# Four graph layers on one core: messages in three bfloat16 parts, one layer turned through DRAM, a new order

## The chip, the cores and the metric

The kernel runs on one core of one Trainium2 chip. The metric is device time in microseconds (us) from the first to the last instruction of one execution. A core has a matrix engine (TensorE, PE in the profile), a vector engine (VectorE, DVE), a scalar engine (ScalarE, ACT), a general engine (GpSimd, POOL) and a queue from which transfers are issued (SyncE, SP). They run side by side and wait for each other on semaphores. Matrix products read their operands from SBUF, the on-chip memory of 128 partitions, and leave their result in PSUM, eight banks of 128 x 512 float32, from where ACT or DVE copy it back.

## The reference

64 graphs of 256 nodes, 256 features each, pass through four layers. Each layer normalises, takes the positive part, runs a graph layer on it and adds the result to x:

```python
h = jnp.maximum(_layernorm(x, axis=-1), 0.0)
x = x + layer(h, adj, ...)
```

Layer 0 is attention of 8 heads, layer 1 attention with one score per edge and a softmax over the other axis, layer 3 attention of 4 heads. Layer 2 is a gated graph network of three rounds, which the change touches most:

```python
A = (adj != 0).astype(x.dtype)
h = x
for i in range(3):
    m = jnp.einsum('bnd,de->bne', h, weight[i])
    aggr = jnp.einsum('bst,bsd->btd', A, m)
    h = _gru_cell(aggr, h, w_ih, w_hh, b_ih, b_hh)
# _gru_cell, with gi = aggr @ w_ih.T + b_ih and gh = h @ w_hh.T + b_hh in three parts:
r = sigmoid(i_r + h_r); z = sigmoid(i_z + h_z)
n = tanh(i_n + r * h_n)
h = (1.0 - z) * n + z * h
```

Everything is float32. The adjacency comes as int32 and holds 0 and 1.

## The kernel before

The kernel works on pairs of graphs, 32 of them, T = 4 tiles of 128 nodes each. Every step is a task with the tiles that it reads and writes, the engines that could do it and an estimated duration; a planner (class Plan) walks through the tasks as a list scheduler would, gives each a place in the order of an engine and a buffer of its pool, and several pairs are thereby in work at once. Only the order comes from it: on the chip, the semaphores decide.

```python
SPARE, GRAIN = 4, 0.001
PERIOD, REST = 138.279, 1.02081
ON_PE = (-212.355, -45.5106, 229.667, -1085.75)      # by layer, added to a task's key
...
base = t.rank[0] * self.PERIOD - rest * self.REST + t.rank[1] * 1e-4
...
key = (round(begin / self.GRAIN), t.key, t.index)    # the ready task with the least key is next
```

Pools, with the number of buffers and how many are kept for the oldest pair: "x" (6, 0), "w4" (28, 9) of 128 x 1024 float32, "mask" (4, 1) of 128 x 1024 bfloat16, "ps" (8, 2), the PSUM banks.

A matrix product needs features on the partitions, the normalisation nodes, so tiles are turned. There are two ways. PE turns 128 x 128 blocks into a bank, and ACT or DVE copy it out. Or DVE turns 32 x 32 blocks in place, and a transfer to DRAM and four back put the blocks where they belong; the tile that comes back is "mixed": the eight 128-blocks lie interleaved, element by element, with steps of 8 float32.

```python
def by_dma(what, p):
    return 0 < p < B // 2 - 1

def through_dram(e, eT):
    d = buf("turn")
    add((SP, 0.6, lambda: nc.sync.dma_start(d(), e())), reads=[e], writes=[d], latency=4.6)
    for b in range(4):
        add((SP, 0.55, ...), reads=[d], writes=[(eT, b)], latency=3.8)

def chunk(hT, k, t):
    if hT.mixed:
        return hT().rearrange("p (n x) -> p x n", x=2 * T)[:, T * k + t]
    ...
```

In the middle 30 pairs the normalised tile of all four layers goes through DRAM (with the scaling and the positive part on ACT, L522), and so does the state between the rounds of layer 2. In the first and last pair DVE scales (L527), PE turns (L542), and the positive part is taken in the copy out of the bank.

Layer 2's messages multiply the state by the adjacency, both float32 (the loaded int32 adjacency is turned into float32 in place):

```python
for o in range(2):
    ps = bank()
    def product(o=o, ps=ps):
        for g in range(2):
            for c in range(2):
                t = 2 * g + c
                mm(ps()[:, g * N : (g + 1) * N], chunk_of(h, t, o), tok(am(), N)[:, t, :],     # L934
                   start=c == 0, stop=c == 1)
```

In rounds 0 and 1 the part h_n stays in its PSUM bank until r is known (pshn): tanh of the half on ACT (L969), then on DVE r = 0.5 * tanh + 0.5 (L974), then (h_n + b) * r out of the bank (L978). The gates' products are L957, those of the last round L1047.

Layer 1 adds its turned mask to the scores on DVE (L856), takes the row maximum (L861), and ACT takes the exponential (L590). Layers 0 and 3 do addition and minimum in one fused DVE step (`lowered`, L655), whose exponentials are L663. The softmax rows of layer 0 are divided on ACT or DVE (L745), its value projection and output projection are L576, layer 1's projection L820, layer 3's L1129; layer 3 spreads a row through DRAM to all partitions (`to_all`), takes Prelu rows (L1150), and multiplies by the turned probabilities (L1172), whose result is turned back (L1187).

Of the kernel before, what the change touches and what calls it, by code (L numbers as in the profile page):

```python
# [9 lines left out]
FP = mybir.dt.float32  # L10
# [12 lines left out]
class Buf:  # L23


    def __init__(self, tag, tiles):
        self.tag, self.tiles, self.slot, self.parts = tag, tiles, None, {}
        self.woven = False
        self.mixed = False
# [9 lines left out]
class Plan:  # L39
# [14 lines left out]
    SPARE, GRAIN = 4, 0.001  # L54
    PERIOD, REST = 138.279, 1.02081
    ON_PE = (-212.355, -45.5106, 229.667, -1085.75)
    ON_SP = (1007.6, 146.333, -62.4427, 928.914)
    OTHERS = (294.968, 127.685, -2183.49, 1293.66)
# [47 lines left out]
    def order(self):  # L106
# [11 lines left out]
        for t in reversed(every):  # L118
            rest = max((x.rest + 0.2 for x in t.after), default=0.0) + min(f[1] for f in t.forms) + t.latency
            t.rest = rest  # L120
            base = t.rank[0] * self.PERIOD - rest * self.REST + t.rank[1] * 1e-4
            engine = t.forms[0][0]
            t.key = base + (self.ON_PE if engine == "PE" else self.ON_SP if engine == "SP" else self.OTHERS)[t.layer]
# [9 lines left out]
        while ready:  # L133
            best = None
            for t in ready:
                start = 0.0
                new = [b.tag for b in t.bufs if b.slot is None]
                for tag in set(new):
                    n = new.count(tag)
                    have = slots[tag]  # L140
                    if len(have) < n + (spares.get(tag, 0) if t.pair != oldest else 0):
                        break
                    start = max(start, have[n - 1][0])
                else:
                    for form in t.forms:
                        engine = form[0]
                        begin = max(start, free.get(engine, 0.0), free.get("port", 0.0) if len(form) > 3 else 0.0)
                        for x in t.before:
                            begin = max(begin, x.end + (self.HOP if x.engine != engine else self.SAME)[x.engine])
                        key = (round(begin / self.GRAIN), t.key, t.index)  # L150
                        if best is None or key < best[0]:
                            best = (key, t, form, begin)
# [9 lines left out]
            t.end, t.engine = begin + us + t.latency, engine  # L162
# [19 lines left out]
def tile_adj_preln_d4(  # L182
# [41 lines left out]
        "x": (6, [P, T * D], FP, 0),  # L224
        "w4": (28, [P, T * D], FP, 9),
# [40 lines left out]
    brz, bih_sb, bhh_sb = held("brz", [P, 4]), held("bih_sb", [P, 6]), held("bhh_sb", [P, 6])  # L266
# [19 lines left out]
    def w4():  # L286
        return buf("w4")
# [91 lines left out]
    def weights2():  # L379
# [45 lines left out]
        def halved():  # L425
            nc.vector.tensor_add(brz, bih_sb[:, 0:4], bhh_sb[:, 0:4])
            nc.vector.tensor_scalar_mul(brz, brz, 0.5)

# [55 lines left out]
    def by_dma(what, p):  # L484

        return 0 < p < B // 2 - 1

    def norm_relu_T(xt, p, tokens=False):
# [15 lines left out]
        def rstd():  # L504
            nc.gpsimd.tensor_scalar_add(rs()[:, 0, :], mv()[:, :, 1], EPS)  # L505
            nc.gpsimd.tensor_tensor(rs()[:, 0, :], rs()[:, 0, :], mhalf, ALU.pow)

        add((G, 1.4, rstd, True), reads=[mv], writes=[(rs, 0)])
        xn, mixed = w4(), by_dma(plan.layer, p)
        relu = tokens or mixed  # L510
        if relu:
            add(
                (V, 0.17, lambda: nc.vector.scalar_tensor_tensor(  # L513
                    rs()[:, 1, :], mv()[:, :, 0], -1.0, rs()[:, 0, :], ALU.mult, ALU.mult)),
                reads=[mv, (rs, 0)], writes=[(rs, 1)],
            )
        for g in range(2):

            def scaled(g=g):
                for t in (2 * g, 2 * g + 1):  # L520
                    if relu:
# [10 lines left out]
            add((A, 0.95, scaled) if relu else (V, 0.7, scaled, True), reads=[(xt, g), mv, rs], writes=[(xn, g)])  # L532
# [4 lines left out]
        for k in range(2):  # L537
            ps = bank()

            def turn(k=k, ps=ps):  # L540
                for t in range(T):
                    nc.tensor.transpose(ps()[:, t * P : (t + 1) * P], tok(xn())[:, t, k * P : (k + 1) * P], ident)  # L542

            add((PE, 4 * TURN, turn), reads=[xn], writes=[ps], claims=[hT])
            dst = lambda k=k: tok(hT(), N2)[:, k, :]
            if tokens:
                add(evict(N2, dst, ps), reads=[ps], writes=[(hT, k)])
            else:
                add(
                    [  # L550
                        (A, act(N2), lambda dst=dst, ps=ps: nc.scalar.activation(dst(), ps(), AF.Relu)),
                        (V, dve(N2), lambda dst=dst, ps=ps: nc.vector.tensor_scalar_max(dst(), ps(), 0.0)),
                    ],
                    reads=[ps], writes=[(hT, k)],
                )
# [29 lines left out]

    def exp_group(e, mx, zs, parts, nm):

        def do():
            for i, m, z in parts:
                nc.scalar.activation(  # L590
                    tok(e(), N)[:, i, :], tok(e(), N)[:, i, :], AF.Exp,
                    bias=mx()[:, m : m + 1], accum_out=zs()[:, z : z + 1],
                )
        return (A, 0.494 * len(parts), do)
# [190 lines left out]
    def to_all(row, src, columns, n, dsts):  # L785
# [8 lines left out]
            (SP, 0.7, lambda: nc.sync.dma_start(row().rearrange("(c p) -> c p", p=P), rows()[0:n, :])),  # L794
# [11 lines left out]
    def layer1(xt, p):  # L806
# [45 lines left out]
        for g in range(2):  # L852
            two = slice(2 * g, 2 * g + 2)
            parts = [(e, 2 * g), (e, 2 * g + 1)]
            add(
                (V, dve(N2), lambda two=two: nc.vector.tensor_tensor(  # L856
                    tok(e(), N)[:, two, :], tok(e(), N)[:, two, :], psm()[:, two, :], ALU.add)),
                reads=[psb], writes=parts,
            )
            add(  # L860
                (V, dve(N2), lambda two=two: nc.vector.tensor_reduce(  # L861
                    mx()[:, two], tok(e(), N)[:, two, :], AX.X, ALU.max, negate=True)),
                reads=parts, writes=[(mx, g)],
            )
            add(exp_group(e, mx, zs, [(i, i, i) for i in (2 * g, 2 * g + 1)], f"1_{p}"), reads=[(mx, g)], writes=[*parts, (zs, g)])
# [39 lines left out]
    def layer2(xt, p):  # L905
        at, hT, h = norm_relu_T(xt, p, tokens=True)
        am = at
        add(
            (V, dve2(T * N), lambda: nc.vector.tensor_scalar(am(), am().bitcast(I32), 0.0, None, ALU.not_equal), True),
            reads=[hT], writes=[am],  # L910
# [8 lines left out]
        def chunk_of(h, t, o):  # L919
            if h.mixed:  # L920
                return h().rearrange("p (m x) -> p x m", x=2 * T)[:, T * o + t]
            return tok(h())[:, t, o * P : (o + 1) * P]

        def messages(h):
            aT = w4()
            aT.woven = woven
            for o in range(2):
                ps = bank()

                def product(o=o, ps=ps):  # L930
                    for g in range(2):
                        for c in range(2):
                            t = 2 * g + c
                            mm(  # L934
                                ps()[:, g * N : (g + 1) * N], chunk_of(h, t, o), tok(am(), N)[:, t, :],
                                start=c == 0, stop=c == 1,
                            )

                add((PE, 1.9 if h.mixed else 1.76, product), reads=[h, am], writes=[ps], claims=[aT])
# [6 lines left out]
        for l in range(NL - 1):  # L946
# [16 lines left out]
            pshn = [gate(1.72, ((whhT, hT),), (4 + o) * P, o, [r, hn]) for o in range(2)]  # L963
            aT = messages(h)
            both = ((whhT, hT), (giT[:, l], aT))
            for o in range(2):
# [7 lines left out]
                    (V, dve2(N2), lambda o=o, r=r: nc.vector.tensor_scalar(at_o(r, o), at_o(r, o), 0.5, 0.5, ALU.mult, ALU.add), True),  # L974
                    writes=[(r, o)],
                )
                add(
                    (V, dve(N2) + 0.07, lambda o=o, ps=pshn[o], r=r, hn=hn: nc.vector.scalar_tensor_tensor(  # L978
                        at_o(hn, o), ps(), bhh_sb[:, 4 + o : 5 + o], at_o(r, o), ALU.add, ALU.mult)),
                    reads=[pshn[o], (r, o), BN], writes=[(hn, o)],  # L980
# [138 lines left out]
    def layer3(xt, p):  # L1119
        at, hT = norm_relu_T(xt, p)  # L1120
        mb = buf("mask")
        add((V, 2 * dve2(N2), lambda: masked_keys(mb, at, ALU.not_equal, 1.0), True), reads=[at, hT], writes=[mb])
        f = buf("f3")
        for t in range(T):
# [6 lines left out]
            add((PE, 0.96 if hT.mixed else 0.9, product), reads=[hT, W3], writes=[ps], claims=[f])  # L1131
# [6 lines left out]
        add(  # L1138
            (V, 0.09, lambda: nc.vector.tensor_copy(dst(), f()[:, :, D + H3 : E3]), True), reads=[f], writes=[dst]
        )  # L1140
        to_all(buf("row3"), dst, lambda: dst().rearrange("p t h -> p (t h)"), T * H3, sd)
# [58 lines left out]

    for p in range(B // 2):
# [8 lines left out]
        if p == 0:  # L1210
            for plan.rank, weights in ((None, weights0), (0.5, weights1), (1.5, weights2), (2.5, weights3)):
                weights()
            plan.rank = None
# [43 lines left out]
```

## Time and profile before

| | before |
|---|---|
| time, median of 3 | 3811.62 us (3810.75 to 3811.85) |
| span of the profiled execution | 3809.6 us |
| busy PE, DVE, ACT, POOL | 3703.2, 3140.9, 2282.9, 687.5 us |
| messages L934: matmul records, mean duration | 1536, 398 ns |
| block turns on DVE for normalised tiles and states (L630) | 360, 1110 ns each |
| writes of tiles to be turned to DRAM, 512 KB each | 564 |
| DMA over the span | 743.00 MB, mean 195 GB/s |

The page gives each engine's busy time and its share of the span. A line such as L934 is a line of the kernel before. In a table of groups the columns are: line, engine, operation, tiles out and in, shapes, count; then total busy time and mean duration in ns; then the idle time of the engine ahead of these instructions, and who ended it. Matmul durations overlap, since the engine is pipelined, and a float32 product leaves two records; transposes leave one. In a timeline the columns are start, duration, engine, line and so on, with idle time ahead of the row in brackets. A table of stretches gives, for each, its length, then busy time and instructions of each engine, the granted PE clock, the DMA share and GB/s.

### The profile page before, as it was taken

To read this page: it belongs to the slowest core of one execution; us is meant where nothing else is said; L and a number is where in the kernel's file an instruction comes from. 1 tells how busy PE (TensorE), PEld (TensorE's weight loads), DVE (VectorE), ACT (ScalarE), POOL (GpSimd) and SP (SyncE) were. 2 spreads that over 40 slices of the span, in tenths; PEclk is the share of its full clock that TensorE was granted. 3 is DMA by queue.
4 is the path that set the end of the run, shared out by engine and by line. 5 is a ranking of instruction groups with operands and counts; after the bars stand their busy time and mean duration, and the time that the engine had idled before them with its cause. 6 is when DMAs were issued, how large, how long until landed. Compare 5 with 4: busy or idle time off the path is not lost. (4 is left out here: it accounts for less than half of the span.)

```text
span 3809.6 us, 54273 instructions
## 1 busy us (share of the span) xinstructions
PE 3703.2 (97%) x15632; PEld 2423.5 (64%) x15632; DVE 3140.9 (82%) x8350; ACT 2282.9 (60%) x6061; POOL 687.5 (18%) x635
## 2 busy tenths in 40 slices
PE   7999999999999999999999999999999999999995
PEld 4665766666666656666666666666666666766663
DVE  7998888788888768888879978898888898887565
ACT  5776556565575655665656656556656556655444
POOL 2001221112211112121221121221111221121121
PEclk9999999999999999999999999999999999999997
DMA  8766574666765757567576666666676676665434
GB/s 266 223 196 198 163 230 159 199 214 179 231 216 158 220 155 217 183 197 235 165 219 206 203 198 185 213 217 195 199 218 201 202 223 198 200 208 161 125 100 127
DMA packets 531801, 743.00 MB, mean 195 GB/s; under 512 B 54704, under 2 KB 446768, under 8 KB 531504
## 3 DMA queue, kind: packets, MB, share of 16 engines
q1 hardware_dynamic: 531504, 739.53, 63.1%
q8 instruction: 126, 2.06, 0.2%
q14 instruction: 171, 1.40, 0.1%
HBM read 426.52 MB, written 312.80 MB: 194 GB/s over the span
## 5 line engine op out<-in xcount | busy, mean ns | idle before, releaser
L663 ACT ACTIVATE w<-w,mx 128x256 f32<-128x256 f32 x1536 | 757.4, 497 | 32.3 <-DVE mx L655 32.0
L957 PE MATMUL ps<-w,whhT 128*128 128x512 f32 x1536 | 710.5, 595 | 1.2 <-ACT w L316 0.8
L957 PE MATMUL ps<-w,giT 128*128 128x512 f32 x1536 | 710.0, 593 | 0.0
L316 ACT COPY w<-ps 128x512 f32<-128x512 f32 x400 | 335.9, 846 | 353.8 <-PE ps L687 86.2
L957 PEld LDWEIGHTS ps<-w,giT 128*128 128x128 f32 x1536 | 290.1, 190 | 348.8 <-issue 333.6
L957 PEld LDWEIGHTS ps<-w,whhT 128*128 128x128 f32 x1536 | 286.8, 191 | 302.7 <-issue 281.8
L621 DVE STREAM_TRANSPOSE w<-w 128x1024 f32<-128x1024 f32 x384 | 460.9, 1223 | 9.4 <-ACT w L663 7.1
L655 DVE CUSTOM_DVE_ANT_0 w<-ps,mask 128x256 f32<-128x256 f32 x1024 | 368.6, 418 | 108.1 <-PE ps L714 105.7
L630 DVE STREAM_TRANSPOSE w<-w 128x512 f32<-128x512 f32 x360 | 374.4, 1110 | 39.3 <-ACT w L522 36.6
L934 PE MATMUL ps<-w,w 128*128 128x256 f32 x1536 | 381.0, 398 | 2.9 <-DMA w<-turn 2.3
L934 PEld LDWEIGHTS ps<-w,w 128*128 128x128 f32 x1536 | 346.8, 280 | 52.5 <-issue 26.0
L1047 PE MATMUL ps<-whhT,w 128*128 128x512 f32 (+1 forms) x1024 | 374.8, 502 | 0.3 <-DVE w L1012 0.3
L1047 PE MATMUL ps<-giT,w 128*128 128x512 f32 (+1 forms) x1024 | 364.0, 495 | 0.6 <-ACT w L316 0.6
L522 ACT ACTIVATE w<-x,rs 128x256 f32<-128x256 f32 x488 | 254.1, 589 | 163.5 <-DVE rs L513 144.3
L1047 PEld LDWEIGHTS ps<-giT,w 128*128 128x128 f32 x1024 | 276.1, 310 | 73.2 <-issue 8.5
L1047 PEld LDWEIGHTS ps<-whhT,w 128*128 128x128 f32 x1024 | 274.0, 311 | 70.8 <-issue 12.2
L663 ACT ACTIVATION_READ_ACCUMULATOR w<-w,mx 128x1 f32 x1536 | 291.6, 190 | 0.0
L1102 POOL TENSOR_TENSOR w<-w,w 128x512 f32<-128x512 f32 x64 | 101.7, 1594 | 1051.8 <-DMA w<-turn 477.2
L994 POOL TENSOR_TENSOR w<-w,w 128x512 f32<-128x512 f32 x128 | 178.7, 1402 | 461.2 <-ACT w L989 406.1
L1150 ACT ACTIVATE w<-w,f 128x256 f32<-128x256 f32 x512 | 216.8, 498 | 27.0 <-DMA w<-row 24.2
L505 POOL TENSOR_SCALAR rs<-mv 128x4 f32<-128x4 f32 x128 | 36.6, 286 | 971.9 <-DVE mv L497 855.9
L655 DVE CUSTOM_DVE_ANT_0 w<-w,mask 128x256 f32<-128x256 f32 x512 | 192.5, 421 | 20.5 <-ACT w L1150 20.5
(120 smaller groups left out, 5706.0 us busy)
## 6 DMA issues: line engine op xcount, KB each, us to landing
turn<-w SPq DMA_DIRECT2D x564, 512.0 KB
w<-turn SPq DMA_DIRECT2D x2256, 128.0 KB
w<-in_adj_dram SPq DMA_DIRECT2D x128, 512.0 KB
w<-row SPq DMA_DIRECT2D x64, 512.0 KB
x<-in_x_dram SPq DMA_DIRECT2D x64, 256.0 KB
out_dram<-x SPq DMA_DIRECT2D x64, 256.0 KB
w<-row SPq DMA_DIRECT2D x32, 256.0 KB
w<-in_L_gnn_weight_dram SPq DMA_DIRECT2D x3, 256.0 KB
```

The source lines that it names most:

```text
L316: (A, act(n), lambda: nc.scalar.copy(dst(), src())),
L522: nc.scalar.activation(tok(xn())[:, t, :], tok(xt())[:, t, :], AF.Relu, bias=rs()[:, 1, t : t + 1], scale=rs()[:, 0, t : t + 1],)
L621: add((V, dve(T * N), lambda: nc.vector.transpose(blocks(), blocks())), writes=[e])
L630: nc.vector.transpose(e().rearrange("p (b i k t) -> p k b t i", b=4, i=32, k=2)[:, k], src().rearrange(f"p {order} -> p k b t j", b=4, j=3 ...
L655: nc.vector.tensor_tensor_reduce(row, src, mask, scale, 3.0e38, ALU.add, ALU.min, mn)
L663: nc.scalar.activation(row, row, AF.Exp, bias=mn()[:, r : r + 1], scale=-1.0, accum_out=zs()[:, z0(r) : z0(r) + 1])
L934: mm(ps()[:, g * N : (g + 1) * N], chunk_of(h, t, o), tok(am(), N)[:, t, :], start=c == 0, stop=c == 1,)
L957: mm(ps(), w[:, k, c0 : c0 + P], wide(src, k), start=n == 0, stop=n == 2 * len(terms) - 1)
L994: either(lambda eng, o=o, u=u, hT=hT, hn=hn: eng.tensor_sub(*((tok(at_o(u, o), T), wide(hT, o), tok(at_o(hn, o), T)) if hT.mixed else (at_ ...
L1047: mm(out, chunk(src, k, t), w[:, k, c0 : c0 + n], start=m == 0, stop=m == 2 * len(terms) - 1)
L1102: either(lambda eng, g=g: eng.tensor_sub(two(df, g).rearrange("p t (k m) -> p t k m", k=2), state(h, g), two(hn, g).rearrange("p t (k m) - ...
L1150: (A, act(N, 1), lambda t=t, g=g, h=h, e=e, r=r: nc.scalar.activation(rows_of(e())[:, r].rearrange("p b (c j) -> p c b j", c=2), sd[g]().r ...
```

## The change

It has five parts.

**Messages.** A float32 is split exactly into three bfloat16 parts: its own upper half, the upper half of what remains, and the upper half of what then remains. The adjacency of 0 and 1 is exact in bfloat16. Three bfloat16 products per chunk take the place of one float32 product. The parts are read in place with a step (`upper`), and two subtractions of 1024 elements on DVE make the remainders. The adjacency is now a bfloat16 "mask" tile.

**Turns.** Only layer 2's tile and its states go through DRAM, there for the first pair too; layers 0, 1 and 3 are turned on PE in all pairs.

**The gate n in rounds 0 and 1.** h_n is taken out of its bank at once as 0.5 * h_n + 0.5 * b, on ACT or DVE; then a single DVE step makes (tanh + 1) * that. L974 goes.

**Layer 1** uses the fused step for mask and minimum.

**Order.** New constants; latencies of transfers count 1.3 times in the plan; a task of SP counts 0.6 us later after another engine; a task with a choice of engines counts 1 us later on DVE and 1.1 us later on POOL; x has 5 buffers and w4 29. The last pair's layer 3 is prepared graph by graph ("fine"). Weights of later layers come at other ranks.

The core of the diff:

```diff
-    SPARE, GRAIN = 4, 0.001
-    PERIOD, REST = 138.279, 1.02081
+    SPARE, GRAIN = 4, 0.01
+    SLOW, MARGIN = 1.3, 0.6
+    BACK = {"DVE": 1, "POOL": 1.1}
+    PERIOD, REST = 133.7, 0
 ...
+                        back = self.BACK.get(engine, 0.0) if len(t.forms) > 1 else 0.0
+                        key = (round((begin + back) / self.GRAIN), t.key, t.index)
 ...
-        "x": (6, [P, T * D], FP, 0),
-        "w4": (28, [P, T * D], FP, 9),
+        "x": (5, [P, T * D], FP, 0),
+        "w4": (29, [P, T * D], FP, 9),
 ...
     def by_dma(what, p):
-        return 0 < p < B // 2 - 1
+        return p < B // 2 - 1 and what in (2, (2, 0), (2, 1))
 ...
+        def upper(ap):
+            return ap.bitcast(BF).rearrange("p (i h) -> p i h", h=2)[:, :, 1]
 ...
         def messages(h):
+            rest = [w4(), w4()]
+            add((V, dve(T * N), lambda: nc.vector.tensor_tensor(
+                in_order(rest[0](), False), in_order(h(), h.mixed), in_order(upper(h()), h.mixed), ALU.subtract), True), ...)
+            add((V, dve(T * N), lambda: nc.vector.tensor_tensor(rest[1](), rest[0](), upper(rest[0]()), ALU.subtract), True), ...)
 ...
                     for g in range(2):
-                        for c in range(2):
-                            t = 2 * g + c
-                            mm(ps()[:, g * N : (g + 1) * N], chunk_of(h, t, o), tok(am(), N)[:, t, :], ...)
+                        for i in range(3):
+                            part = (h, *rest)[i]
+                            for c in range(2):
+                                t = 2 * g + c
+                                mm(ps()[:, g * N : (g + 1) * N], chunk_of(part(), part.mixed, t, o), tok(am(), N)[:, t, :], ...)
 ...
-            pshn = [gate(1.72, ((whhT, hT),), (4 + o) * P, o, [r, hn]) for o in range(2)]
+            for o in range(2):
+                ps = gate(1.72, ((whhT, hT),), (4 + o) * P, o, [r, hn])
+                add([(A, act(N2, 1), ... AF.Identity, bias=bhn[:, o : o + 1], scale=0.5),
+                     (V, dve(N2), ... tensor_scalar(at_o(hn, o), ps(), 0.5, bhn[:, o : o + 1], ALU.mult, ALU.add))], ...)
 ...
-                    (V, dve2(N2), ... tensor_scalar(at_o(r, o), at_o(r, o), 0.5, 0.5, ALU.mult, ALU.add), True),
-                    (V, dve(N2) + 0.07, ... scalar_tensor_tensor(at_o(hn, o), ps(), bhh_sb[...], at_o(r, o), ALU.add, ALU.mult)),
+                    (V, dve(N2), ... scalar_tensor_tensor(at_o(hn, o), at_o(r, o), 1.0, at_o(hn, o), ALU.add, ALU.mult), True),
 ...
+            def logits(g=g):                       # layer 1
+                for t in (2 * g, 2 * g + 1):
+                    row = tok(e(), N)[:, t, :]
+                    lowered(row, row, psm()[:, t, :], -1.0, mx()[:, t : t + 1])
 ...
+        for ts, sds in ((slice(0, 2), sd[:1]), (slice(2, 4), sd[1:])) if hT.fine else ((slice(0, T), sd),):   # layer 3
 ...
-            for plan.rank, weights in ((None, weights0), (0.5, weights1), (1.5, weights2), (2.5, weights3)):
+            for plan.rank, weights in ((None, weights0), (1.4, weights1), (1.1, weights2), (1, weights3)):
```

## The prediction

> **What bounds the kernel now.** I read the page first, then the table of stretches, then TensorE's own instructions in order of time, then the groups with shapes kept apart.
>
> ```profile
> PE 3703.2 (97%) x15632; PEld 2423.5 (64%) x15632; DVE 3140.9 (82%) x8350; ACT 2282.9 (60%) x6061; POOL 687.5 (18%) x635
> ...
> PEclk9999999999999999999999999999999999999997
> ```
>
> TensorE (PE) is busy 97% of the span, at full clock. The next engine, VectorE (DVE), has 82%. A busy PE may hide slack, so the stretches come next.
>
> ```profile
> core 0: us, PE busy (x) PEld busy (x) DVE busy (x) ACT busy (x) POOL busy (x), PEclk, DMA share, GB/s
> ...
> 2000.00:3000.00 1000.00, 995.65 (x4236) 661.86 (x4235) 869.63 (x2335) 615.83 (x1639) 187.76 (x172) 1.00 0.66 203
> ...
> 3700.00:3810.00 110.00, 67.69 (x269) 39.95 (x267) 60.28 (x142) 43.52 (x122) 14.97 (x13) 0.81 0.41 125
> ```
>
> In the middle PE is 99.6% busy with DVE at 87%: DVE can go that high before PE starves. Only the ends are loose. To learn what a matmul really costs, I subtract the start of each PE row from the start of the next (less the idle time in brackets), since the durations shown overlap. Six rows show how:
>
> ```profile
> 2017.07 3.97 PE L934 MATMUL ps<-w,w 128*128 128x256 f32 x16
> 2020.88 2.07 PE L820 MATMUL ps<-w1a,w 128*128 128x258 f32 x8
> ...
> 2048.64 0.65 PE L1187 MATMUL ps<-ident,w 128*128 128x128 f32 x4
> 2049.13 0.27 PE L789 MATMUL ps<-ident,f 128*4 128x128 f32 x1
> ...
> 2065.17 0.61 PE L846 MATMUL ps<-identb,mask 128*128 128x128 bf16 x8
> 2065.62 1.94 PE L957 MATMUL ps<-w,whhT 128*128 128x512 f32 x4
> ```
>
> The messages (L934), 16 records, take 2020.88 - 2017.07 = 3.81 us. A float32 matmul leaves two records, so that is 8 matmuls at 0.476 us. Four float32 transposes (L1187) take 0.49 us, 0.122 each. Eight bfloat16 transposes of 128 columns (L846) take 0.45 us, 0.056 each. Summed so over the whole timeline, PE's steps come to 3700 us: L934 363.5 (1536 records, 0.237), the value projection with its weight turned through DRAM 0.248 per record against 0.223 for the output projection, whose weight was turned on chip; L820 0.243, L1129 0.244. The other 110 us of the span are idle PE: about 25 in the first 200 us, 42 in the last 110 us, 42 scattered between. (The time is some 2 us above the span.)
>
> **What the Trainium skill says.** (1) "FP8 and Floating Point Precision" (TensorE Precision Notes) says that true float32 takes four passes through the array. The trace agrees: 512 columns at two records of 0.431 us are 0.86 us, which is four times 512 columns at the 2.4 GHz that "TensorE: Matmul & The Clock Gate" gives under "What's actually happening"; L934 without strided weights would be 0.43. (2) That TensorE page, "Weight-path perf modes — Fast Weight Load (FWL) and DoubleRow", says weights that are not float32 load faster when there are 128 of them, with a column step allowed. L846's bfloat16 loads (98 ns against 190 to 334 for float32 ones) agree for packed weights; no run here yet shows strided bfloat16 weights. (3) "SBUF — State Buffer", "Door 1: The DMA port swizzle", speaks of 16-byte lines: each access that crosses to a new line pays. The turned layout has steps of 32 bytes, and the trace agrees:
>
> ```profile
> L621 DVE STREAM_TRANSPOSE w<-w 128x1024 f32<-128x1024 f32 x384 | 460.9, 1223 | 9.4 <-ACT w L663 7.1 <-ACT w L745 2.0
> L630 DVE STREAM_TRANSPOSE w<-w 128x512 f32<-128x512 f32 x360 | 374.4, 1110 | 39.3 <-ACT w L522 36.6 <-DMA w<-turn 1.9
> ...
> L527 DVE TENSOR_SCALAR w<-x,mv,rs 128x256 f32<-128x256 f32 x24 | 11.2, 524 | 1.9 <-POOL rs L506 1.8
> ```
>
> Half the elements (L630) take nearly the time of the packed transpose (L621).
>
> **The change, part by part, on PE.** *Messages.* Per pair 3 layers x 2 halves x 2 graphs x 3 parts x 2 chunks = 72 bfloat16 matmuls of 256 columns, 2304 in all. Twice L846's 0.056 is 0.112 us; 2304 x 0.112 = 258 us in place of 363.5: **-105 us**. If the strided weight loads pace them at 0.135, it is 311 us and -52. *Transposes back on PE.* Layers 0, 1 and 3 of 30 pairs, 8 each, 720 x 0.125 = **+90 us**; the first pair's layer 2 goes through DRAM now, 24 x 0.125 = **-3**. *Packed weights again* in those layers: 480 records of the value projection x (0.248 - 0.223) = 12, of L820 x 0.018 = 9, of L1129 x 0.014 = 7, **-28 us**. Sum: -46, PE's work goes from 3700 to about 3654 us. So most of what the cheap matmuls save is paid out again in transposes.
>
> **On DVE.** Removed: 174 of the strided L630 transposes x 1.11 = -193; the shift terms of L513, 90 x 0.2 = -19; L974, 128 x 0.427 = -55; layer 1's add and maximum (41 + 41) become 128 fused steps of 0.42 + 0.08, -18; copies of q and k out of the banks no longer interleave (median 1.07 us, against about 0.68 packed), some -20. Added: 360 scaled rows x 0.39 (the median of L527 is 0.408; its mean holds a few long ones) = +140; the two remainders of each message, 192 subtractions of 1024 elements. L896, two float32 operands and 512 elements, has a median of 0.686, so 1024 are about 1.25 us, and 62 of them read with a 32-byte step, perhaps 2 us: +240 to +300. Sum about +110. Then the new weight BACK counts a flexible step on DVE as 1 us later than one on ACT: I expect about half of L745's 708 DVE instances and a third of the evictions to go to ACT, -150, while the new evictions (180 relu'd halves, 128 of hn) go mostly to ACT, +30 on DVE. DVE ends near 3130 us, as before. ACT loses the relu of 360 scaled rows (-211) and gains the evictions (+180) and half of L745 (+150): about 2400. Neither reaches PE's 3654, so this lies beside PE's work. The shorter r chain and banks freed early take nothing off a PE that already has work waiting.
>
> **DMA** writes of turned tiles fall from 564 to 477; PE waits for them were only a few tens of us in all, so this is worth little in the middle.
>
> **The ends.** In the last pair PE waits 27.3 us for layer 3's turned probabilities, while ACT does 16 Prelu rows (6.5 us) and then 16 exponentials (7.9 us) one after the other for both graphs. Split by graph, the first graph's share can start earlier, but the last graph still waits for its row through DRAM, its exponentials and the turn: I take **-8 us**. The margins for DMA latency should trim the scattered 42 us: **-7**. The moved weights at the start: 0. Sum: 3811.6 - 46 - 8 - 7 = **3750 us**, 1.6% less.
>
> **Rivals.** *A: the bfloat16 matmuls are paced by weight loads or by issue.* For: two of the six weights in a group have a 32-byte step, and the float32 loads of that layout pace L934 now (0.237 per record against 0.215 of streaming). Against: L846 keeps 0.056 with 128 columns only, twice as dense as needed. It gives about 3800 us. *B: DVE becomes the bound.* For: the remainders cost 250 us or more, on the chain between two layers of the GRU, and the middle already shows 87%. If nothing shifts to ACT and the strided reads take 2.2 us, DVE has about 3350 us; then PE idles 100 us more and the time is 3800 to 3850 us. Against: the removed L630 and BACK. *C: the new order is much better.* If the scattered idle nearly goes, the ends give 25 us and the matmuls stream at 0.107: 3700 us. *D: buffers.* Remainders take two more w4 tiles per message and layer 2 holds a mask tile through three layers, of four; x falls to five. Waits for buffers would show as PE idle in the middle; the plan counts them, so I give 10%.
>
> **Range and chances.** PE's sum is the firmest part, within about 40 us either way, mostly from the bfloat16 rate. Idle time is free within about -40 to +60. I take 3695 to 3805. The 2% line is at 3735; the centre is 15 us above it, with a spread of some 43: 0.35 for faster. Slower by 2% would need over 120 us of new idle on top of the gain: 0.05.
>
> **What would show it.** PE's busy time some 45 us lower; L934's successor near 0.112 per matmul with 2304 records; about 750 more transposes on PE at 0.12 to 0.13; L630 at 186 instances; DVE near 3130 and ACT near 2400; PE over 97% in the middle. DVE well over 3300 with PE gaps that end on DVE would mean rival B; L934 steps over 0.13, rival A. A time under 3700 would mean that idle PE, or steps that I count as PE's work, held more hidden waiting than I read.

## The result

The changed kernel takes 3771.21 us (median of 4 executions, 3767.03 to 3776.0). The ratio to the kernel before is 0.9893, with a 95% interval of 0.9876 to 0.9911: 40 us less, where the prediction had 62 less (3750) and a range of 3695 to 3805.

Lines are now those of the changed kernel: messages L965 (before L934), gates L988 and L1084 (L957, L1047), turns on TensorE L555 (L542), scaling on DVE L537 (L527), projections L592, L826, L1166 (L576, L820, L1129), division L751 (L745). The page of the changed kernel:

```profile
span 3769.1 us, 56446 instructions
...
PE 3679.7 (98%) x17097; PEld 2308.8 (61%) x17097; DVE 3093.9 (82%) x7982; ACT 2521.8 (67%) x6756; POOL 594.1 (16%) x543
...
PE 29%; DVE 21%; ACT 14%; DMA 5%; issue 2%; SPq 2%; POOL 1%; POOLq 0%; DVEq 0%; ACTq 0%
...
L636 DVE STREAM_TRANSPOSE w<-w 128x512 f32<-128x512 f32 x186 | 197.3, 1122 | 10.6 <-ACT w L532 10.6
L537 DVE TENSOR_SCALAR w<-x,mv,rs 128x256 f32<-128x256 f32 x384 | 165.7, 484 | 47.9 <-POOL rs L517 47.9
...
turn<-w SPq DMA_DIRECT2D x477, 512.0 KB, 3.0
```

The instruction counts are as predicted (186, 384, 477), DVE's total too. The third line quoted is the chain that ended last, by engine, as shares of the whole span. It could be followed back only to 997 us, so the shares add up to 74%: of the part that was followed TensorE has 39%, DVE 28%, ACT 19%. The table of stretches and six rows of TensorE's timeline, same kernel:

```profile
2000.00:3000.00 1000.00, 996.48 (x4672) 624.57 (x4665) 846.67 (x2209) 694.28 (x1873) 168.16 (x149) 1.00 0.61 178
...
3650.00:3770.00 120.00, 86.30 (x344) 50.72 (x343) 71.52 (x166) 49.77 (x133) 10.41 (x12) 0.83 0.36 103
```

```profile
1516.58 2.84 PE L965 MATMUL ps<-mask,w 128*128 128x256 bf16 x24
1519.26 0.60 PE L1228 MATMUL ps<-ident,w 128*128 128x128 f32 x4
...
1560.36 1.04 PE L555 MATMUL ps<-ident,w 128*128 128x128 f32 x8
1561.23 1.88 PE L693 MATMUL ps<-w,wk_sb 128*128 128x512 f32 x4
...
1566.44 1.54 PE L555 MATMUL ps<-ident,w 128*128 128x128 f32 x8
1567.82 0.27 PE L795 MATMUL ps<-ident,f 128*4 128x128 f32 x1
```

From start to start, 24 bfloat16 matmuls take 2.68 us, 0.112 each. Eight transposes take 0.87 us in one place and 1.38 in another, with no idle time noted between them: a wait hides inside the second row (for what, the weight loads tell further down). Added up over the timeline as in the prediction, in the span of the profiled executions:

| | before | after | difference | predicted |
|---|---|---|---|---|
| messages | 363.8 | 258.5 | -105 | -105 |
| transposes for tiles and states | 12.9 | 120.6 | +108 | +87 |
| projections with packed weights | 377.2 | 343.4 | -34 | -28 |
| other steps of PE | 2949 | 2961 | +12 | 0 |
| idle PE | 106 | 86 | -21 | -15 |
| span | 3809.6 | 3769.1 | -40 | -61 |

("Other" and idle are what remains to the sums of steps, 3703 and 3684 us, and to the span; the prediction cut the timeline elsewhere and had 3700 and 110.)

### The profile page after: what moved, and what is told of

It is laid out like the page before. It is cut to its first block, busy times and chain, and to the rows that moved or that the text cites. A ratio compares the mean times of both kernels' runs of the same rounds, so it can differ in the third digit from the quotient of the medians.

```text
span 3769.1 us, 56446 instructions
## 1 busy us (share of the span) xinstructions
PE 3679.7 (98%) x17097; PEld 2308.8 (61%) x17097; DVE 3093.9 (82%) x7982; ACT 2521.8 (67%) x6756; POOL 594.1 (16%) x543
## 4 chain that ended last, share of the span: by engine, by line
PE 29%; DVE 21%; ACT 14%; DMA 5%; issue 2%; SPq 2%; POOL 1%; POOLq 0%; DVEq 0%; ACTq 0%
PE ps L988 11%; ACT w L669 5%; PE ps L1084 5%; DMA w<-turn 5%; DVE st L502 3%; DVE w L537 3%; PE ps L1166 2%; PE ps L965 2%; ACT w L1191 2%; PE ps L592 2%; DVE w L627 2%; DVE w L636 2%; DVE w L1146 1%; SPq L619 1%; PE ps L720 1%
## 5 line engine op out<-in xcount | busy, mean ns | idle before, releaser
L988 PE MATMUL ps<-w,whhT 128*128 128x512 f32 x1536 | 728.6, 601 | 3.8 <-DMA w<-turn 3.6
L988 PE MATMUL ps<-w,giT 128*128 128x512 f32 x1536 | 708.9, 593 | 0.2 <-ACT w L322 0.2
L322 ACT COPY w<-ps 128x512 f32<-128x512 f32 x518 | 386.3, 765 | 344.6 <-PE ps L592 151.8
L988 PEld LDWEIGHTS ps<-w,giT 128*128 128x128 f32 x1536 | 288.9, 190 | 351.2 <-issue 331.9
L988 PEld LDWEIGHTS ps<-w,whhT 128*128 128x128 f32 x1536 | 276.8, 191 | 301.9 <-issue 282.6
L751 ACT ACTIVATE w<-w,rz 128x256 f32<-128x256 f32 x910 | 387.9, 505 | 5.0 <-DVE rz L744 3.4
L1084 PE MATMUL ps<-whhT,w 128*128 128x512 f32 (+1 forms) x1024 | 375.6, 504 | 0.1
L1084 PE MATMUL ps<-giT,w 128*128 128x512 f32 (+1 forms) x1024 | 364.3, 494 | 0.0
L1084 PEld LDWEIGHTS ps<-giT,w 128*128 128x128 f32 x1024 | 281.7, 312 | 74.5 <-issue 5.1
L1084 PEld LDWEIGHTS ps<-whhT,w 128*128 128x128 f32 x1024 | 274.5, 317 | 64.2 <-issue 14.8
L669 ACT ACTIVATION_READ_ACCUMULATOR w<-w,mx 128x1 f32 x1536 | 309.4, 201 | 0.0
L1031 POOL TENSOR_TENSOR w<-w,w 128x512 f32<-128x512 f32 x91 | 121.7, 1338 | 1168.8 <-ACT w L1026 1077.8
L965 PE MATMUL ps<-mask,w 128*128 128x256 bf16 x2304 | 272.0, 274 | 4.0 <-DVE mask L917 2.9
L965 PEld LDWEIGHTS <-w 128*128 128x128 bf16 x2304 | 231.3, 108 | 70.9 <-issue 45.7
L1117 ACT ACTIVATE w<-w 128x512 f32<-128x512 f32 x128 | 80.2, 627 | 192.0 <-DVE w L1113 190.9
L636 DVE STREAM_TRANSPOSE w<-w 128x512 f32<-128x512 f32 x186 | 197.3, 1122 | 10.6 <-ACT w L532 10.6
L537 DVE TENSOR_SCALAR w<-x,mv,rs 128x256 f32<-128x256 f32 x384 | 165.7, 484 | 47.9 <-POOL rs L517 47.9
```

Of the source, the lines that this page charges most:

```text
L322: (A, act(n), lambda: nc.scalar.copy(dst(), src())),
L537: nc.vector.tensor_scalar(tok(xn())[:, t, :], tok(xt())[:, t, :], mv()[:, t, 0:1], rs()[:, 0, t : t + 1], ALU.subtract, ALU.mult,)
L636: nc.vector.transpose(e().rearrange("p (b i k t) -> p k b t i", b=4, i=32, k=2)[:, k], src().rearrange(f"p {order} -> p k b t j", b=4, j=3 ...
L669: nc.scalar.activation(row, row, AF.Exp, bias=mn()[:, r : r + 1], scale=-1.0, accum_out=zs()[:, z0(r) : z0(r) + 1])
L751: op(row, row, rz()[:, r : r + 1])
L965: mm(ps()[:, g * N : (g + 1) * N], chunk_of(part(), part.mixed, t, o), tok(am(), N)[:, t, :], start=i == 0 and c == 0, stop=i == 2 and c == 1,
```

## The experiments

Theory P, the prediction's: TensorE's work sets the time, and DVE lies beside it. Rival L: each engine works in a fixed order, and a loop of waits through DVE, ACT, TensorE and DRAM closes once per pair of graphs; this loop is about as long as TensorE's work, so neither alone sets the time. The first four kernels start from the changed one.

**E1, one part only.** TensorE does a third of the message products; order, DVE and all else as they were.

```diff
-                        for i in range(3):
+                        for i in range(1):
-                                    start=i == 0 and c == 0, stop=i == 2 and c == 1,
+                                    start=i == 0 and c == 0, stop=c == 1,
```

> The changed kernel, same order of instructions, but the messages multiply only the first bfloat16 part: 1536 of 2304 products are left out (the remainders are still computed and not used, so the output is coarse). If TensorE is the bound, its work falls by 1536 x 0.112 = 172 us and the time to about 3600, at most 3640 us. If the DVE chain (remainders, scaling) sets the pace, the time stays above 3700.

Measured: 3772.65 us (3767.91 to 3777.61), ratio to before 0.9892 (0.9877 to 0.9908): nothing gained. The stretch and then a part of its chain of waits, in order of time:

```profile
2000.00:3000.00 1000.00, 963.36 (x4218) 583.58 (x4206) 844.50 (x2202) 691.13 (x1860) 166.81 (x148) 0.98 0.61 177
```

```profile
2104.10 5.75 DMA w<-turn
2109.86 1.19 DVE w L951
2111.05 0.60 DVE w L1113
...
2168.38 1.97 ACT w L669 x8
...
2187.78 5.15 PE ps L988 x12
...
2217.78 5.71 DMA w<-turn
2223.52 1.22 DVE w L951
2224.74 0.60 DVE w L1113
```

TensorE dropped to 96% in the middle, DVE kept its 84 to 85%. The chain passes the same two DVE steps, after the same transfer from DRAM, 113.7 us later (2223.52 - 2109.86), and goes through ACT and TensorE in between. Thirty-two such rounds are 3637 us, most of the span. (Any steady order repeats once per pair; what tells is that TensorE has 31% of the chain as far as it was followed, DVE 30%, ACT 29%.) The message steps fell by 165 us; TensorE's idle time in the middle rose from 15 to 114 us, and the other steps grew by 55. Four rows of TensorE's timeline and one stretch show how this hangs together:

```profile
2168.18 1.88 PE L988 MATMUL ps<-w,giT 128*128 128x512 f32 x4
2169.90 1.04 PE L965 MATMUL ps<-mask,w 128*128 128x256 bf16 x8
...
2176.88 3.37 PE L988 MATMUL ps<-w,giT 128*128 128x512 f32 x4 [2.95 <-ACT w L322]
2180.05 4.19 PE L1084 MATMUL ps<-whhT,w 128*128 128x256 f32 x16
```

```profile
2177.00:2181.00 4.00, 4.00 (x7) 1.96 (x8) 4.00 (x8) 4.00 (x13) 0.00 (x0) 0.57 0.49 190
```

Once in most pairs TensorE waits some 2.9 us for a copy by ACT out of a bank (L322; 70.6 us in all between 400 and 3660 us), and then four matmul records take 3.17 us from start to start instead of 1.72, while the granted clock (0.57 over this stretch, 1.00 over the 7 us before) is low. Between 400 and 3660 us there are 23 such times of 3.4 or 6.8 us at half the clock; the changed kernel has none there. Steps that began in them took about 41 us more than the same steps elsewhere (an estimate from this trace), most of the 55. So the null result has a brake in it: 68 us of TensorE's pieces of the chain lie in these times, and at an even clock E1 might have been some 30 us faster, again an estimate. But 114 us of TensorE's time in the middle are idle, and P, which asks for 3600 to 3640, falls: TensorE's work by itself does not hold the changed kernel at 3771.

**E2, no subtractions.** DVE loses the remainders, TensorE keeps its 2304 products, all on the first part.

```diff
-  (V, dve(T * N), lambda: nc.vector.tensor_tensor(rest[1](), rest[0](), upper(rest[0]()), ALU.subtract), True),
+  (V, dve(T * N), lambda: None, True),          # and rest[0] likewise
-  part = (h, *rest)[i]
+  part = h
```

> The changed kernel, same order, but the two subtractions that make the remainders are left out and all three products use the first part (the output is coarse). DVE loses 285 us, TensorE's work stays. If TensorE is the bound, the time stays within 15 us of 3771. If DVE is the bound or its chain sets the pace, the time falls by over 60 us. Side question: all six weights of a group now have the 32-byte step in rounds 1 and 2; if such loads pace the matmuls, a step of L965's successor rises from 0.112 to 0.13 or more.

Measured: 3722.56 us (3721.91 to 3726.98), ratio 0.9763 (0.9749 to 0.9778): 49 us below the changed kernel. A little less than expected of a bound DVE, far more than P allows. Its chain by engine, and its stretch:

```profile
PE 66%; ACT 29%; DVE 3%; issue 1%; DMA 1%; SPq 0%; POOL 0%; ACTq 0%; POOLq 0%; DVEq 0%
```

```profile
2000.00:3000.00 1000.00, 998.86 (x4721) 634.99 (x4718) 799.97 (x2173) 701.81 (x1883) 168.23 (x153) 1.00 0.63 183
```

This chain reaches back to the start, so its shares can be set beside those of the followed part before: DVE fell from 28% to 3%, and TensorE has hardly a gap (6 us in the middle). Its steps add up to 3645 us with the same number of instructions as the changed kernel's 3684: of those 39 us, 26 were waits inside transposes, which take 0.119 us here and 0.152 there. What E2 takes away is three things at once: DVE's work, the two steps between a state's return from DRAM and its products, and the use of two w4 tiles; it does not part them. The side question: the loads of message weights fall into two groups, 98 ns and 143 ns (medians); in numbers these fit the weights with a 4-byte and with a 32-byte step. The slower group grows from 507 of 2304 loads in the changed kernel to 1488 here, and a message matmul still takes 0.111 us. Rival A of the prediction is out.

**E3, float32 messages.** The rest of the change stays.

```diff
-        am = buf("mask")
+        am = at
-                        for i in range(3): ...                     # bfloat16 parts
+                        for c in range(2): mm(..., chunk_of(h, t, o), tok(am(), N)[:, t, :], ...)
```

> The changed kernel with the messages undone: float32 products, adjacency in float32, no remainders. TensorE gains about 105 us of work, DVE loses 285. If TensorE is the bound: 3850 to 3880 us. If DVE is the bound: less than 3820.

Measured: 3888.22 us (3885.67 to 3890.33), ratio 1.0193 (1.0176 to 1.021): 117 us above the changed kernel, 8 above the range. With DVE relieved (2862 us) the time follows TensorE's steps: they add up to 3782 us, 98 more; idle TensorE grows by some 20. So the cheap messages do pay, in this surrounding.

**E4, everything through DRAM.** Layers 0, 1 and 3 of the middle pairs turned through DRAM, as before.

```diff
-        return p < B // 2 - 1 and what in (2, (2, 0), (2, 1))
+        return p < B // 2 - 1 and (p > 0 or what in (2, (2, 0), (2, 1)))
```

> The changed kernel with the turns of layers 0, 1 and 3 through DRAM again in the middle 30 pairs. TensorE loses 720 transposes (720 x 0.15 = 108 us with their hidden waits) and pays some 28 us for weights with steps: about 80 us less work. If TensorE is the bound and the rest still fits beside it: about 3690 us, faster than both kernels. If the turns were moved back because DVE, buffers or the way through DRAM could not keep up any more: 3771 us or more, with new idle TensorE that ends on DMA or DVE.

Measured: 3914.63 us (3907.59 to 3916.43), ratio 1.0261 (1.0246 to 1.0277): 143 us slower than the changed kernel. The 109 us of transposes are gone, but TensorE's steps still add up to 3670: strided projections are back (L1166 0.255 us a record), and steps at half the clock cost about 40 us in the middle (estimated as for E1). Idle TensorE in the middle is 160 us, spread over copies on ACT, DRAM, the last step of a state (L1049) and the remainders (L951, L946). Whether the turns had to move for the bfloat16 messages in any order, or in this one only, E4 does not tell.

The next three go from the two ends: one part alone in the kernel before, and the old order under the new work.

**E5, the kernel before with the messages alone.** Diff as in the front part: `messages`, `upper`, and the mask tile; nothing else.

> The kernel before with only the messages changed (three bfloat16 parts, two subtractions, bfloat16 adjacency in a mask tile). If TensorE alone is the bound: 105 us less, about 3707. If the chain through DVE, ACT and the way through DRAM closes a loop about as long as TensorE's work, as the run with one part suggests: no gain, 3812 or more, up to 3950, with idle TensorE in the middle.

Measured: 4155.02 us (4148.75 to 4160.26), ratio 1.0887 (1.0871 to 1.0903), 341 us slower than the kernel before, and 205 above the most that was expected of a loop. Page, and who TensorE waited for (us in total, times, longest):

```profile
PE 3721.4 (90%) x16400; PEld 2348.9 (57%) x16400; DVE 3380.1 (81%) x8479; ACT 2320.4 (56%) x6146; POOL 661.0 (16%) x613
```

```profile
PE ps L1193 <- DMA w<-turn: 128.6, 20, 26.5
PE ps L764 <- DMA w<-turn: 28.5, 16, 5.8
PE ps L955 <- DVE w L941: 26.4, 15, 5.9
PE ps L955 <- DVE w L936: 25.4, 7, 9.2
```

No engine is over 90% busy. TensorE waits for layer 3's probabilities from DRAM (L1193), up to 26.5 us at a time, and for the remainders themselves. DVE has 3380 us of 4156, so it is not full either. That is what L would look like, but which loop closes is not shown: the chain of this run could be followed only over its last 490 us. Some 85 us of TensorE's steps in the middle are the half clock again (estimated as for E1), so waits cost more here than their own length.

**E6, the kernel before with the turns alone.**

```diff
-        return 0 < p < B // 2 - 1
+        return p < B // 2 - 1 and what in (2, (2, 0), (2, 1))
```

> The kernel before with only the turns changed (layers 0, 1 and 3 turned on TensorE again, layer 2 through DRAM in the first pair too). TensorE gains 720 transposes at 0.12 (86 us) less 28 us for packed weights and 3: if it is the bound, 3812 + 55 to 3812 + 75, about 3875. If the loop through DVE and DRAM is the bound of the kernel before, a shorter loop: 3812 or less.

Measured: 3879.3 us (3875.08 to 3883.61), ratio 1.0165 (1.015 to 1.018). TensorE's steps add up to 3765, 61 more, and the time follows by 65. Here P holds, as in E3: in both, DVE has no remainders to make, and the time follows TensorE's steps.

**E7, the changed kernel in the old order.**

```diff
-    SLOW, MARGIN = 1.3, 0.6
-    BACK = {"DVE": 1, "POOL": 1.1}
-    PERIOD, REST = 133.7, 0
+    PERIOD, REST = 138.279, 1.02081       # offsets, GRAIN, ranks, x 6 and w4 28 as before
+    SLOW, MARGIN, BACK = 1.0, 0.0, {}
```

> The changed kernel with the old order's constants: no margins, no BACK, latencies as they are, the old offsets by layer, ranks and buffer counts. If TensorE's work alone sets the time, the order matters little: 3771 within 25 us, DVE near 3250 since flexible steps go to it again. If a loop across engines, fixed by the order, sets the pace: 3810 or more, with new idle TensorE in the middle.

Measured: 4083.81 us (4080.73 to 4090.33), ratio 1.0703 (1.0687 to 1.0719): 313 us slower for the order alone (with one buffer of x against one of w4, and the flexible steps where this order puts them). DVE does 3291 us, and TensorE waits 134.1 us for layer 3's turned probabilities, as in E5; steps at half the clock cost about 61 us in the middle (estimated as for E1).

**E8, the last pair's layer 3 as a whole.**

```diff
-        ..., plan.layer == 3 and p == B // 2 - 1      # fine
+        ..., False
```

> The changed kernel with the last pair's layer 3 prepared as a whole again. From the traces the stretch from the last gate product to the end is 61.6 us before and 52.7 us after: 8 to 9 us slower, about 3780, if the split is what shortened it; 3771 if something else did.

Measured: 3784.78 us (3784.04 to 3787.56), ratio 0.9917 (0.99 to 0.9933), whose interval overlaps that of the changed kernel a little. The stretch from the last gate product to the end is 61.8 us, as before the change, against 52.7. The split gives about these 9 us; the other 4 or so are not explained, and the changed kernel's own executions lie 9 us apart.

Then the order alone. The instructions of E9, E11 and E12 are those of the changed kernel, but which of ACT, DVE or POOL does a flexible step can differ.

**E9, another order.** The plan is told durations from the traces and has other constants.

```diff
-    SLOW, MARGIN = 1.3, 0.6
-    BACK = {"DVE": 1, "POOL": 1.1}
+    SLOW, MARGIN = 1.193, 1.215
+    BACK = {"DVE": 0.379, "POOL": 1.509}
-    ON_PE = (940, -967, 1371, -841)                   # and PERIOD, REST, ON_SP, OTHERS
+    ON_PE = (946.9, -729.8, 1371.0, -373.9)
-            add((A, 0.95, scaled) if shift else (V, 0.7, scaled, True), ...
+            add((A, 1.02, scaled) if shift else (V, 0.8, scaled, True), ...
-        add((V, 2 * dve(N2), blocks), reads=[src], writes=[e])
+        add((V, 2.03, blocks), reads=[src], writes=[e])
-                (V, dve(T * N), ...                   # the first remainder
+                (V, 1.95 if h.mixed else 1.19, ...
 ...
```

> The changed kernel, the same instructions, another order: the plan is told the durations that the traces show (scaling 0.8 us, a state's block turn 2.03, the first remainder 1.95 from a turned state, and so on), and has other constants. If the loop across engines that the order fixes holds the changed kernel at 3771, it falls: TensorE's work without the hidden waits is about 3645 us, with 65 us of loose ends 3710, so 3700 to 3740, faster than both kernels. If TensorE's work alone sets 3771, it stays within 20 us of that.

Measured: 3769.09 us (3764.31 to 3771.91), ratio 0.9872 (0.9849 to 0.9895), no better than the changed kernel. The expected gain did not come. **E10, one part in that order**, with the edit of E1:

> The same order as the run before it, but the messages multiply the first bfloat16 part alone (1536 products left out, coarse output). In the order of the changed kernel leaving these out gained nothing. If the new order leaves TensorE as the bound, part of the 172 us comes out now: 40 us or more below the run before it. If a loop still closes at the same length: within 15 us of it.

Measured: 3713.24 us (3711.34 to 3714.82), ratio 0.9727 (0.9706 to 0.9748), 56 us below E9. The chain by engine of E9:

```profile
PE 81%; DMA 7%; DVE 6%; ACT 3%; SPq 2%; issue 1%; POOL 0%; DVEq 0%; POOLq 0%; ACTq 0%
```

So the same removed work is worth nothing in one order and 56 us in another of the same length, though DVE does more in the second (3176 us against 3094): what binds depends on the order, not on the load alone. Part of the difference can be the clock: steps at half the clock cost an estimated 41 us in the middle of E1 and 24 in E10. In E9 TensorE holds 81% of the chain, but it has 45 us of idle time in the middle, half of it for turned tiles from DRAM. The 24 us won inside its steps (3684 to 3660) were lost there.

**E11, the changed kernel's constants with the measured durations.**

> The changed kernel with the measured durations in its plan and its own constants. If the plan's too short DVE durations cause the waits (transposes on TensorE that wait 0.3 us for their scaled rows), the time falls to about 3735 and a transpose's step from 0.152 to 0.13 or less. If the constants were fitted to the plan as it is, any other order is worse: above 3780.

Measured: 3769.97 us (3769.35 to 3771.18), ratio 0.9877 (0.9851 to 0.9902). Half of what was expected: the transposes' hidden waits go (0.152 to 0.119 us, 26 us in all), but the time does not, as idle TensorE grows from 86 to 112 us. The waits moved. Neither of the two ends of the expectation was met: the order is no better and no worse.

**E12, without BACK.**

```diff
-    BACK = {"DVE": 1, "POOL": 1.1}
+    BACK = {}
```

> The changed kernel without BACK: a flexible step goes where it can begin first. DVE gets about 150 us more work (3240), ACT less. If DVE is in the loop that sets the pace, slower: 3800 to 3850. If DVE lies beside TensorE as the prediction had it: 3771 within 15 us.

Measured: 3824.22 us (3819.74 to 3829.06), ratio 1.0021 (1.0015 to 1.0028), 53 us slower than the changed kernel. DVE does 3248 us, 155 more, while TensorE's steps (3679 us) are hardly changed. TensorE's idle time in the middle grows from 15 to 78 us, and the longest of its waits between 400 and 3713 us are for DVE:

```profile
PE ps L965 <- DVE w L951: 12.6, 12, 2.0
PE ps L555 <- DVE w L537: 9.3, 11, 3.0
PE ps L988 <- DVE w L1049: 8.9, 5, 5.4
```

In the changed kernel L965 waits 1.0 us for the remainder (L951). So DVE's load is on the path. (BACK also moves steps in the order; load and order were not parted.) Without BACK the gain of the whole change is gone.

## Why the prediction was right, and where its reasons were not

**The messages** cost what the bfloat16 transposes of the mask promised: 0.112 us each, -105 us. The Trainium skill, "TensorE: Matmul & The Clock Gate", "Weight-path perf modes — Fast Weight Load (FWL) and DoubleRow", allows a column step. The trace adds a price, 143 ns a load with the 32-byte step against 98, and E2 shows that such loads do not pace the matmuls: 0.111 us each.

**Packed weights** gave 34 us for 28. **Idle time**: the split of the last layer gave the 8 to 9 us (idle TensorE in the last 110 us went from 42 to 33), but the start lost 11 (27 us in the first 400 before, 38 after), and the middle gained more than the 7 that the prediction gave it, 37 to 15.

**The transposes** were mis-sized: 108 us for 87. The price of a transpose, 0.125 us, was near where little waits (0.119 us in E2 and E11). What was missing is that a tile scaled on DVE has to be ready: TensorE's loads waited 182 times for L537, about 0.3 us each:

```profile
PEld ps L555 <- DVE w L537: 58.5, 182, 7.3
```

**The step that failed** is "Neither reaches PE's 3654, so this lies beside PE's work". Busy time was near the mark (DVE 3094 for 3130), the 85% of the middle is below the 87% that the kernel before bore, and still DVE's work counts: less of it gains 49 us (E2), more of it costs 53 (E12). In place of an engine beside the path, E1 and E2 show DVE's steps on a chain with ACT's and TensorE's. A busy share tells whether an engine has room, not whether its steps come in time; "DVE can go that high before PE starves" was read from the kernel before, in another order. The trace of the changed kernel has a hint: TensorE is 99.6% busy in the middle, but has 39% of the chain that could be followed. It is no more than a hint, since E9 and E11 took as long with 81% and 78%. The Trainium skill, "Perfetto Trace Analysis", "Identifying the Most-Contended Engine", says that matmul busy time is not a good measure of how close one is to the roofline, because matmuls are pipelined; this case adds another reason, 26 us of waits inside transposes that count as busy.

**The rivals.** B had the right engine for the wrong reason: DVE did not fill up (3094 us, not 3350), its steps stood on the chain. C's hope (3700) was not met by two other orders, E9 and E11. Two sizes beside the path were off as well: 594 of the 708 divisions on DVE went to ACT, not half, and those 240 more at 0.505 us come to 121 us, about what ACT (2522 us) has above 2400. Groups by shape, changed kernel:

```profile
L751 ACT ACTIVATE w<-w,rz 128x256 f32<-128x256 f32 x910 | 387.9, 505 | 5.0 <-DVE rz L744 3.4
...
L946 DVE TENSOR_TENSOR w<-w 128x1024 f32<-128x1024 f32 x96 | 168.0, 1750 | 8.4 <-DMA w<-turn 7.5 <-ACT w L322 0.6
L951 DVE TENSOR_TENSOR w<-w 128x1024 f32<-128x1024 f32 x96 | 116.6, 1215 | 0.3
```

**The total** came near because the errors were small and partly cancelled: 21 us of transposes and 12 of other steps, less 6 each from packed weights and idle time, are the 21 us by which 3771 lies above 3750. That a sum of TensorE's work comes so near is in part luck: in this order the other chain is about as long, and the prediction had no means to know that. Applied to one part alone the same reasoning fails badly: it gives 3707 for the messages in the kernel before, and E5 took 4155.

**Left open.** In E5 and E7 the remainders' time, the tighter pool of w4 tiles and the old order act together; they were not parted. The gate n taken early and layer 1's fused step were not run alone. That DVE, ACT and TensorE hold each other up is seen in E1 and E2; what an even clock would have made of E1, and whether an order of this work can be shorter, is not shown. E2, with 3645 us of steps and 70 us of idle ends, says that some 3720 us is what TensorE's own work needs in this order.

## What to carry to other kernels

When two engines are both over 80% busy and every engine's order is fixed, take work off each in turn before believing that one is the bound: here 172 us off TensorE gave nothing, 285 us off DVE gave 49, and in a different order the same 172 us gave 56. A cheaper operation that lays new work on another engine may need a new order: the same messages cost 341 us in the old one. Read a step from start to start: waits hide in rows that count as busy. And when work is taken off an engine, compare the granted clock and the steps that were left alone: in E1 part of what was saved came back as slower matmuls.

## What the runs showed of the hardware

A subtraction of 1024 float32 with a 32-byte step takes 2.0 us (median) against 1.2 packed (L946, L951), as the Trainium skill, "SBUF — State Buffer", "Door 1: The DMA port swizzle", would have it for accesses that each cross to a new line. Weight loads of bfloat16 with this step take 143 ns against 98, but stay hidden: 0.111 us a matmul in E2. And taking two thirds of the message products away lowered the mean granted clock of TensorE from 0.990 to 0.978: in E1 23 times of 3.4 or 6.8 us at half the clock lie between 400 and 3660 us, 21 of them beginning within 1.5 us of the end of a wait of 2.6 to 3.0 us; the changed kernel has none there. A record of a 512-column float32 matmul (L988) took 0.853 us from start to start within such times, 0.429 outside (medians).
